# Four score banks shared by all lanes, and softmax numerators formed by a second, transposed product

## The chip, the core and the metric

The kernel runs on one core of a Trainium2 chip. The metric is the time of the whole kernel on the device in microseconds (us), the median of several runs; lower is better. The profile is one further execution, recorded by the hardware profiler. Its engines are named PE (TensorE matmuls), PEld (TensorE weight loads), DVE (VectorE), ACT (ScalarE), POOL (GpSimd) and SP (SyncE, which here issues most DMAs).

## The reference, cut to what matters

Four blocks run one after the other over 32 sequences of 64 tokens with 256 features; every attention has 16 heads of 16 features.

```python
# block 0: queries from x, keys from ctx and x (128 keys), integer key mask on the ctx half
attn = where(full_mask, einsum('bkhd,bnhd->bhkn', q, kmat) / 16, -inf)
x = mlp(rmsnorm(softmax(attn) @ v @ out_w + out_b + x)) + x
# block 1: a recurrent time mix (a scan over 64 steps) and a channel mix; no attention
# block 2: self attention, then cross attention on ctx (64 keys each), then an MLP
scores = einsum('bhqd,bhkd->bhqk', q, k) / 4
scores = scores * mask - 10000.0 * (1.0 - mask)
out = einsum('bhqk,bhkd->bhqd', softmax(scores), v)
# block 3: cross attention with a boolean key mask, gated
scores = where(mask, einsum('bhtd,bhsd->bhts', Q, K) / 4, -inf)
x = x + tanh(gate) * (softmax(scores) @ V @ Wo.T)
```

## The kernel before, in words

The 32 sequences are cut into 8 groups of 4 sequences (256 tokens). A job is one block applied to one group, so there are 32 jobs. Four lanes (class `Lane`, L83) each run one job at a time. A job is a Python generator; the loop at L1235 goes round the lanes and advances each by one `yield`, which sets the priority of the instructions that it emits. A scheduler then places the instructions on each engine's queue by priority and by when it believes that they can start; each queue is worked off in that fixed order. `next_job` (L1194) lets at most two lanes be in block 1, starts block 2 once every group has started block 0, and block 3 once every group has started block 2.

Each lane owns 11 working tiles of 128 x 512 (`s` and `d`) and two of the eight PSUM banks (`BANKS`, L58). Every product that a lane forms takes one of its two banks and gives it back when ACT or DVE has read it. The projections go through `matmul` (L203): most multiply a pair of high and low parts by three products of 128 x 256 (L210), some are plain fp32 (L207).

The 16 heads of an attention are taken as c (2) x r (4) x j (2). The keys are stored block-diagonally: one 32-row strip of the features holds two heads (j), and `bd_keys` (L369) writes each key tile twice, masked by `ind`, so that a product over the strip gives the scores of both heads side by side. The queries hold two strips per 64-row half, and `queries` (L340) writes them twice, each time masked by `par` so that one strip is zero. The product for r then runs over the 64 rows of `half_rows(r)`, half of them zeros.

`attention64` (L449, blocks 2 and 3) makes for each r: a bank of scores (16 fp32 matmuls as PE sees them, L460; in block 3 ahead of them a mask product of two rows, L1161), and `softmax_unit` (L409): a maximum per row over the keys (DVE, L414), a subtraction (DVE, L416), four 128 x 128 transposes (PE, L422), and the exponential (ACT, L424). In block 2 the mask is applied by a DVE multiplication (L1097) and a POOL addition (L1098) ahead of that. The scores of r + 1 are asked for before the unit of r, and there is a `yield` after each r. Then come the sums (L479), the reciprocals, the product with the values (L489) and the output projection. Block 0 does the same inside `block0` (L569) with its own score function (mask product L648, scores L655), sums (L673) and values (L687), twice per job (i = 0, 1). Queries of block 0 are evacuated by four activations (L609). `key_mask` (L549) loads the key mask with one DMA and turns it into 0 or -1e30 in bf16 on two rows.

An attention use is one pass through this for one group (or for one i in block 0). There are 16 uses in block 0, 16 in block 2 and 8 in block 3.

Of the kernel before, what the change touches and what calls it, by code (L numbers as in the profile page):

```python
# [38 lines left out]
ALU = mybir.AluOpType  # L40
# [17 lines left out]
BANKS = (2, 2, 2, 2)  # L58
# [58 lines left out]
def kernel(ctx: ExitStack, tc: tile.TileContext, a: dict, out: bass.AP):  # L117
# [4 lines left out]
    lanes = [Lane(ctx, tc, n) for n in range(NL)]  # L122

# [15 lines left out]
    make_identity(nc, ident)  # L139
    eps5 = mk(const, [P, 1], "eps5")  # L140
# [22 lines left out]
    def feat2(t):  # L163
        return t[:, :512].rearrange("p (c t) -> p c t", c=NC)
# [64 lines left out]
    par = mk(const, [P, 2], "par")  # L229
    nc.scalar.dma_start(out=par, in_=a["par"])  # L230
    half_bf = mk(const, [2, P], "half_bf", dt=BF16)
    halfT = mk(const, [2, P], "halfT")
    nc.scalar.dma_start(out=halfT, in_=a["half"].rearrange("p j -> j p"))
# [106 lines left out]
    def queries(L, w, src, bias):  # L340


        q = [feat2(L.s()) for _ in range(2)]

        def evac(ps):
            for u in range(2):
                on = par[:, u : u + 1]
                if bias is None:
                    nc.scalar.activation(q[u], ps, AF.Copy, scale=on)
                else:  # L350
                    for c in range(NC):
                        nc.scalar.activation(
                            q[u][:, c, :], ps[:, c, :], AF.Identity, bias=bias[:, c, u : u + 1],
                            scale=on,
                        )

        project_T(L, w, src, evac)
        return lambda r, c, seq: q[r % 2][half_rows(r), c, seq * S : (seq + 1) * S]

    def half_rows(r):  # L360
        return slice(64 * (r // 2), 64 * (r // 2) + 64)
# [17 lines left out]
    def keys64(L, w, src, bias):  # L379

        k = [L.d().rearrange("p (b j s) -> p b j s", b=GB, j=2) for _ in range(NC)]
        project_T(
            L, w, src,
            each(lambda c, ps: bd_keys(
                lambda j: k[c][:, :, j, :], ps.rearrange("p (b s) -> p b s", s=S), c, bias
            )),
        )
        return lambda r, c, seq: k[c][half_rows(r), seq].rearrange("p j s -> p (j s)")
# [20 lines left out]
    def softmax_unit(L, s, n, scale, in_place=False):  # L409

        sv = s.rearrange("p (m n) -> p m n", n=n)
        m = 512 // n
        mx = L.tmp([P, m], "mx")
        nc.vector.tensor_reduce(mx, sv, AX.X, ALU.max)  # L414
        d = s if in_place else L.d()
        nc.vector.tensor_tensor(  # L416
            d.rearrange("p (m n) -> p m n", n=n), sv,
            mx.unsqueeze(2).to_broadcast([P, m, n]), ALU.subtract,
        )
        pt = L.bank("T")  # L420
        for i in range(4):
            nc.tensor.transpose(pt[:, i * P : (i + 1) * P], d[:, i * P : (i + 1) * P], ident)  # L422
        e = L.d()
        nc.scalar.activation(e, pt, AF.Exp, scale=scale)  # L424
        return e
# [23 lines left out]
    def attention64(L, q, k, v, scale, masked):  # L449


        def scores(r):
            sc = L.bank("A")
            begun = masked(sc, False)
            for i in range(2):
                for c in range(NC):
                    for b in range(2):
                        seq = 2 * i + b
                        o = (i * NC + c) * P
                        nc.tensor.matmul(  # L460
                            sc[64 * b : 64 * b + 64, o : o + P],
                            lhsT=q(r, c, seq), rhs=k(r, c, seq),
                            start=not begun,
                            stop=not begun or (i, c) == (1, NC - 1),
                        )
            return sc

        es = []
        sc = scores(0)
        for r in range(4):  # L470
            m, own = masked(sc, True), sc

            sc = scores(r + 1) if r < 3 else None
            es.append(softmax_unit(L, m, S, scale, m is not own))
            yield
        out = L.s()[:, :512].rearrange("p (i n) -> p i n", i=TT)
# [54 lines left out]
    def weights0():  # L531
# [4 lines left out]
        W["qb0"] = masked_bias("l0_qb", par)  # L536
# [12 lines left out]
    def key_mask(L, name, g, dt, width):  # L549

        m = L.tmp([2, TT, S], "m2", dt, 1)
        nc.sync.dma_start(
            out=m,
            in_=a[name][g * GB : (g + 1) * GB, :].rearrange("(i b) k -> b i k", b=2),
        )
        f = L.tmp([2, TT, width], "f2", BF16, 1)
        if width > S:
            nc.gpsimd.memset(f[:, :, S:], 0.0)
        nc.vector.tensor_scalar(f[:, :, :S], m, 0.0, -BIG, ALU.is_equal, ALU.mult)
        return f  # L560

# [7 lines left out]
    def block0(L, g):  # L569
        x = tok2(L.s())  # L570
        nc.sync.dma_start(out=x, in_=token_major(a["x"], g))
        mb = key_mask(L, "mask0", g, mybir.dt.int32, 2 * S)
        ct = None
        for i in range(TT):
# [24 lines left out]
            q = L.d().rearrange("p (u c t) -> p u c t", u=2, c=NC)  # L599
# [7 lines left out]
            for u in range(2):  # L607
                for c in range(NC):
                    nc.scalar.activation(  # L609
                        q[:, u, c, :], ps[:, c, :], AF.Identity, bias=W["qb0"][:, c, u : u + 1],  # L610
                        scale=par[:, u : u + 1],
                    )
# [33 lines left out]
            def scores(r):  # L646
                sc = L.bank("A")
                nc.tensor.matmul(  # L648
                    sc.rearrange("p (m n) -> p m n", m=4), lhsT=half_bf,
                    rhs=mb[:, i, :].unsqueeze(1).to_broadcast([2, 4, P]),  # L650
                    start=True, stop=False,
                )
                for c in range(NC):
                    for b in range(2):
                        nc.tensor.matmul(  # L655
                            sc[64 * b : 64 * b + 64, c * D : (c + 1) * D],
                            lhsT=q[half_rows(r), r % 2, c, b * S : (b + 1) * S],
                            rhs=kk[c][half_rows(r), b].rearrange("p j h s -> p (j h s)"),
                            start=False, stop=c == NC - 1,
                        )  # L660
                return sc

            es = []
            sc = scores(0)
            for r in range(4):
                own = sc
                sc = scores(r + 1) if r < 3 else None
                es.append(softmax_unit(L, own, P, 1.0 / DH))
                yield
# [376 lines left out]
    def weights2():  # L1046
# [4 lines left out]
        W["qb2"] = masked_bias("l2_qb", par)  # L1051
# [8 lines left out]
        W["cqb2"] = masked_bias("l2_cqb", par)  # L1060
# [20 lines left out]
    def block2(L, g):  # L1081
        x = load_x(L, g)
        m2 = L.tmp([P, TT, S], "m2", bufs=1)
        nc.sync.dma_start(
            out=m2,
            in_=a["mask2"][g * GB : (g + 1) * GB, 0].rearrange("(i b) q k -> (b q) i k", b=2),
        )
        f2 = L.tmp([P, TT, S], "f2", bufs=1)
        mask_fill(f2, m2)

        def masked(m, f):
            def fn(sc, done):
                if not done:
                    return False
# [279 lines left out]
```

## Time and profile before

| what | value |
|---|---|
| median of 3 runs (lowest to highest) | 1218.55 us (1217.73 to 1218.82) |
| the profiled execution's own time | 1220.28 us |
| its span | 1218.5 us |
| instructions in the span | 26280 |
| mean granted TensorE clock | 0.951 |
| DMA | 69.83 MB, mean 57 GB/s, 18.1% of the 16 engines' time on the main queue |

The span is the stretch of the profile that all shares refer to. In a group line the two numbers after the bar are the summed busy time in us and the mean duration of one in ns; because TensorE overlaps neighbouring matmuls, the busy time of a matmul group divided by its count is the interval at which matmuls follow each other, and it is smaller than the mean duration. After the second bar stands the idle time of the engine just before the group, and what ended it. TensorE counts an fp32 matmul of the source twice, which is why 768 score products in the source are 1536 matmuls in the profile.

### The profile page before, as it was taken

Reading aid. Unit: us, or ns where it says so; the run is one execution under the profiler, and the core shown is the slowest. Engines: PE = TensorE matmul, PEld = TensorE weight load, DVE = VectorE, ACT = ScalarE, POOL = GpSimd, SP = SyncE. Lnnn points to the kernel's source line nnn. Section 1 sums busy time; section 2 is a strip of 40 time slices with the busy share of each in tenths; the row PEclk is TensorE's granted clock in tenths of the full one; section 3 lists DMA queues with packets and bytes.
Section 4 is the critical chain, followed back from the end, with each engine's and each line's share of the span. In section 5 each row is a group of like instructions: output and inputs, shape, how many; then the busy total and the mean of one; then the engine's idle time right before and its main releaser. Section 6 shows DMA issues by size and latency. Waiting matters only on the chain. (4 is left out here: it accounts for less than half of the span.)

```text
span 1218.5 us, 26280 instructions
## 1 busy us (share of the span) xinstructions
PE 1133.0 (93%) x10524; PEld 876.4 (72%) x10524; DVE 875.9 (72%) x1561; ACT 649.5 (53%) x1288; POOL 449.2 (37%) x553
## 2 busy tenths in 40 slices
PE   6999999979998999987889857999999999999998
PEld 5667879746776767765767634897778897788875
DVE  4646563898679877699877997768887455886456
ACT  5556864444464654434634313665557675456852
POOL 2002131542348423366335754455454232231100
PEclk9999998988999999987889886999999999999999
DMA  7300011341122311232221220101000110101101
GB/s 219 112 23 15 27 52 54 122 130 45 53 63 90 102 41 56 61 100 70 90 69 52 76 66 29 45 27 36 21 21 18 37 36 18 45 28 45 61 2 36
DMA packets 76953, 69.83 MB, mean 57 GB/s; under 512 B 10361, under 2 KB 73119, under 8 KB 76831
## 3 DMA queue, kind: packets, MB, share of 16 engines
q1 hardware_dynamic: 76140, 68.10, 18.1%
q8 instruction: 83, 1.36, 0.5%
q14 instruction: 40, 0.32, 0.1%
q10 hardware_dynamic: 690, 0.05, 0.1%
HBM read 49.51 MB, written 14.68 MB: 53 GB/s over the span
## 5 line engine op out<-in xcount | busy, mean ns | idle before, releaser
L210 PE MATMUL bank<-w,s 128*128 128x256 f32 x1632 | 235.8, 292 | 10.3 <-DVE s L200 4.6
L210 PEld LDWEIGHTS bank<-w,s 128*128 128x128 f32 x1632 | 209.1, 192 | 27.9 <-issue 8.8
L210 PE MATMUL bank<-s,w 128*128 128x256 f32 x1344 | 200.3, 297 | 7.5 <-ACT s L199 4.3
L210 PEld LDWEIGHTS bank<-s,w 128*128 128x128 f32 x1344 | 176.5, 197 | 24.8 <-issue 8.1
L424 ACT ACTIVATE s<-bank 128x512 f32<-128x512 f32 x160 | 95.1, 599 | 138.9 <-PE bank L422 127.4
L200 DVE TENSOR_TENSOR s<-s,s 128x512 fp32r<-128x512 f32 x128 | 102.6, 803 | 84.3 <-ACT s L199 83.5
L1098 POOL TENSOR_TENSOR s<-s,f 128x512 f32<-128x512 f32 x64 | 86.6, 1358 | 132.7 <-DVE s L1097 111.5
L207 PE MATMUL bank<-s,w 128*128 128x256 f32 x448 | 114.1, 399 | 2.7 <-DVE s L819 1.3
L960 POOL TENSOR_TENSOR s<-s,s 128x512 f32<-128x512 f32 x64 | 90.1, 1408 | 71.1 <-DVE s L956 67.8
L422 PE MATMUL bank<-ident,s 128*128 128x128 f32 x640 | 105.1, 289 | 6.5 <-DVE s L416 6.1
L460 PE MATMUL bank<-s,s 64*64 64x128 f32 x1536 | 107.7, 278 | 3.3 <-ACT s L424 1.7
L956 DVE TENSOR_TENSOR_SCAN s<-s,s 128x260 f32<-128x260 f32 x128 | 105.8, 867 | 0.5
L199 ACT CAST s<-s 128x512 fp32r<-128x512 f32 x128 | 79.0, 621 | 50.0 <-DVE s L494 31.4
L460 PEld LDWEIGHTS bank<-s,s 64*64 64x64 f32 x1536 | 82.4, 133 | 27.6 <-issue 14.2
L422 PEld LDWEIGHTS bank<-ident,s 128*128 128x128 f32 x640 | 72.8, 145 | 36.6 <-issue 18.8
L207 PEld LDWEIGHTS bank<-s,w 128*128 128x128 f32 x448 | 84.3, 198 | 20.5 <-issue 4.1
L414 DVE TENSOR_REDUCE mx<-bank 128x4 f32<-128x512 f32 (+1 forms) x96 | 65.3, 683 | 40.5 <-PE bank L655 23.4
L869 POOL TENSOR_TENSOR s<-s,s 128x512 f32<-128x512 f32 x40 | 56.2, 1412 | 76.6 <-DVE s L866 58.3
L655 PE MATMUL bank<-s,s 64*64 64x256 f32 x512 | 74.8, 397 | 0.0
L504 ACT ACTIVATE s<-bank,vecs 128x256 f32<-128x256 f32 x128 | 53.7, 472 | 31.2 <-PE bank L210 30.8
L293 ACT ACTIVATE s<-bank,vecs 128x256 f32<-128x256 f32 x96 | 48.8, 567 | 36.1 <-PE bank L258 35.2
L258 PE MATMUL bank<-ident,s 128*128 128x128 f32 x288 | 50.9, 293 | 18.2 <-DVE s L286 10.6
(156 smaller groups left out, 1969.2 us busy)
## 6 DMA issues: line engine op xcount, KB each, us to landing
s<-vd SPq DMA_DIRECT2D x128, 128.0 KB
s<-xd SPq DMA_DIRECT2D x32, 256.0 KB
xd<-s SPq DMA_DIRECT2D x24, 256.0 KB
cxd<-s SPq DMA_DIRECT2D x32, 128.0 KB
s<-cxd SPq DMA_DIRECT2D x16, 256.0 KB
stage<-in_l_w_dram SPq DMA_DIRECT2D x12, 256.0 KB
s<-s SPq DMA_DIRECT2D x48, 64.0 KB
s<-in_x_dram SPq DMA_DIRECT2D x8, 256.0 KB
```

The costliest lines, as they stand in the source:

```text
L199: nc.scalar.copy(hi, src)
L200: (eng or nc.vector).tensor_tensor(lo, src, hi.bitcast(F32), ALU.subtract)
L207: nc.tensor.matmul(out, lhsT=lf(l), rhs=rf(r), start=start, stop=stop)
L210: nc.tensor.matmul(out, lhsT=lf(l[u]), rhs=rf(r[v]), start=start and n == 0, stop=stop and n == 2)
L414: nc.vector.tensor_reduce(mx, sv, AX.X, ALU.max)
L422: nc.tensor.transpose(pt[:, i * P : (i + 1) * P], d[:, i * P : (i + 1) * P], ident)
L424: nc.scalar.activation(e, pt, AF.Exp, scale=scale)
L460: nc.tensor.matmul(sc[64 * b : 64 * b + 64, o : o + P], lhsT=q(r, c, seq), rhs=k(r, c, seq), start=not begun, stop=not begun or (i, c) == ...
L655: nc.tensor.matmul(sc[64 * b : 64 * b + 64, c * D : (c + 1) * D], lhsT=q[half_rows(r), r % 2, c, b * S : (b + 1) * S], rhs=kk[c][half_rows ...
L956: nc.vector.tensor_tensor_scan(f, wT[:, c].rearrange("p b s -> p (b s)"), f, 0.0, ALU.mult, ALU.add)
L960: nc.gpsimd.tensor_tensor(st, st, per_t(rT[:, c, :]), ALU.mult)
L1098: nc.gpsimd.tensor_tensor(sv, sv, f, ALU.add)
```

## The change

Each lane keeps one PSUM bank of its own, and the other four banks become one tile `sc` that all lanes share. An attention takes the tile whole, and the next user waits until the last one has read it.

The masking of the queries by `par` is gone: the queries are written once, and the product for r runs over its own 32-row strip (`pair_rows`). The four r are the innermost loop, each writing its own bank of `sc`, so that neighbouring matmuls use different strips of rows and different halves of columns of the array.

In blocks 0 and 3 the subtraction, the transposes and the reading of scores for them are gone. Instead `maxima` reduces two banks at a time on DVE, `shifts` splits each maximum into three bf16 parts with four small POOL operations and turns them by one product, which ACT copies to SBUF; `numerators` writes the same four banks again: the mask, the scores with keys and queries exchanged (so that they come out transposed), and the product of `take_off` (a constant of minus ones) with the parts, which takes the maxima off. Then four exponentials read the banks. There are three yields where there were five.

In block 2 all four r are multiplied and masked first, then reduced, subtracted and transposed as before, but into a second use of the shared tile. Its mask tile is loaded later, into a working tile.

`key_mask` now writes the mask to four strips by four DMAs, and the constants for it (zeroed tiles per lane, `half_bf` on four strips, `take_off`, `parts`) are made at the start.

```diff
-BANKS = (2, 2, 2, 2)
+BANKS = (1, 1, 1, 1)
...
+    score_ps = ctx.enter_context(tc.tile_pool(name="score_ps", bufs=1, space=PSUM))
...
     def queries(L, w, src, bias):
-        q = [feat2(L.s()) for _ in range(2)]
+        q = feat2(L.s())
...
+    def score_banks():
+        return mk(score_ps, [P, 4, 512], "sc")
+
+    def maxima(L, mx, src, n):
+        nc.vector.tensor_reduce(mx, src.rearrange("p r (m n) -> p r m n", n=n), AX.X, ALU.max)
+
+    def shifts(L, mx):
+        t = parts[L.n]
+        wide = lambda m: m.to_broadcast([P, 4, 4, 2]) if m.shape[3] == 1 else m
+        rest = L.tmp([P, 4, 4, 2], "rest", bufs=1)
+        nc.gpsimd.tensor_copy(t[:, :, 0], wide(mx))
+        nc.gpsimd.tensor_tensor(rest, wide(mx), t[:, :, 0], ALU.subtract)
+        nc.gpsimd.tensor_copy(t[:, :, 1], rest)
+        nc.gpsimd.tensor_tensor(t[:, :, 2], rest, t[:, :, 1], ALU.subtract)
+        ps = L.bank("T")[:, :P]
+        nc.tensor.matmul(
+            ps, lhsT=t.rearrange("p r u m j -> p (r u m j)"), rhs=ident_bf, start=True, stop=True
         )
+        sh = L.s(BF16)[:, :P]
+        nc.scalar.copy(sh, ps)
+        return sh
+
+    def numerators(L, sc, sh, q, k, scale, mask):
+        for m in range(4):
+            o = m * P
+            for r in range(4):
+                nc.tensor.matmul(
+                    sc[:, r, o : o + P], lhsT=mask(r, m), rhs=half_bf[32 * r : 32 * r + 2],
+                    start=m == 0, stop=False,
+                )
+        for m in range(4):
+            for b in range(2):
+                o = m * P + b * S
+                for r in range(4):
+                    nc.tensor.matmul(
+                        sc[:, r, o : o + S], lhsT=k(r, m, b), rhs=q(r, m, b),
+                        start=False, stop=False,
+                    )
+        for m in range(4):
+            o = m * P
+            for r in range(4):
+                nc.tensor.matmul(
+                    sc[:, r, o : o + P], lhsT=take_off[32 * r : 32 * r + 24, m],
+                    rhs=sh[32 * r : 32 * r + 24], start=False, stop=m == 3,
+                )
+        es = [L.d() for _ in range(4)]
+        for r, e in enumerate(es):
+            nc.scalar.activation(e, sc[:, r], AF.Exp, scale=scale)
+        return es
...
+    def attention64(L, q, k, v, scale, masked=None, key_masks=None):
+        sc = score_banks()
+        if key_masks is not None:
+            begin_masked(
...
+        for i in range(2):
+            for c in range(NC):
+                o = (i * NC + c) * P
+                for b in range(2):
+                    for r in range(4):
                         nc.tensor.matmul(
-                            sc[64 * b : 64 * b + 64, o : o + P],
-                            lhsT=q(r, c, seq), rhs=k(r, c, seq),
+                            sc[64 * b : 64 * b + 64, r, o : o + P],
+                            lhsT=q(r, c, 2 * i + b), rhs=k(r, c, 2 * i + b),
...
+        if key_masks is not None:
+            for r in range(0, 4, 2):
+                maxima(L, mx[:, r : r + 2], sc[:, r : r + 2], S)
+            sh = shifts(L, mx.rearrange("p r (m j) -> p r m j", j=2))
             yield
+            es = numerators(
...
+        else:
+            ds = [masked(sc[:, r]) for r in range(4)]
+            yield
+            for r, d in enumerate(ds):
+                dv = d.rearrange("p (m n) -> p m n", n=S)
+                nc.vector.tensor_reduce(mx[:, r], dv, AX.X, ALU.max)
+                nc.vector.tensor_tensor(
+                    dv, dv, mx[:, r].unsqueeze(2).to_broadcast([P, 8, S]), ALU.subtract
+                )
+            pt = score_banks()
+            es = []
+            for r, d in enumerate(ds):
+                for m in range(4):
+                    nc.tensor.transpose(
+                        pt[:, r, m * P : (m + 1) * P], d[:, m * P : (m + 1) * P], ident
+                    )
+                es.append(L.d())
+                nc.scalar.activation(es[r], pt[:, r], AF.Exp, scale=scale)
+        yield
...
+    def key_mask(L, name, g, dt, both):
...
+        for r in range(4):
+            nc.sync.dma_start(
+                out=m[32 * r : 32 * r + 2],
...
+    def begin_masked(sc, mask, n):
+        for b in range(2):
+            for r in range(4):
+                nc.tensor.matmul(
+                    n(sc[64 * b : 64 * b + 64, r]),
+                    lhsT=half_bf[32 * r : 32 * r + 2, 64 * b : 64 * b + 64],
+                    rhs=mask(r), start=True, stop=False,
+                )
```

Block 0 takes the same route: `begin_masked`, scores over `pair_rows(r)` with r innermost, `maxima`, `shifts`, a yield, `numerators`, a yield.

## The prediction

> **What bounds the kernel now.** I read the page's first two parts first, to see which engine is full and where.
>
> ```profile
> PE 1133.0 (93%) x10524; PEld 876.4 (72%) x10524; DVE 875.9 (72%) x1561; ACT 649.5 (53%) x1288; POOL 449.2 (37%) x553
> PE   6999999979998999987889857999999999999998
> PEclk9999998988999999987889886999999999999999
> ```
>
> TensorE has work in 93% of the span. The kernel has stages, so I then asked for the busy time of each engine in six stretches (PE, PEld, DVE, ACT, POOL, then clock, DMA share, GB/s):
>
> ```profile
> 30.00:200.00 170.00, 168.57 (x1689) 125.34 (x1685) 93.61 (x173) 108.92 (x221) 27.00 (x47) 0.99 0.16 45
> 200.00:330.00 130.00, 120.92 (x844) 86.21 (x845) 98.71 (x172) 58.30 (x119) 50.21 (x63) 0.89 0.28 86
> 330.00:550.00 220.00, 208.30 (x1654) 154.51 (x1653) 176.42 (x303) 105.56 (x215) 108.14 (x125) 0.97 0.24 74
> 550.00:765.00 215.00, 176.43 (x1331) 130.93 (x1331) 184.36 (x299) 91.38 (x173) 111.32 (x120) 0.84 0.20 64
> 765.00:950.00 185.00, 178.30 (x1919) 149.40 (x1919) 138.42 (x263) 114.23 (x224) 92.45 (x100) 0.99 0.09 28
> 950.00:1198.00 248.00, 246.90 (x2746) 203.47 (x2745) 158.12 (x297) 149.97 (x295) 53.63 (x72) 0.99 0.11 33
> ```
>
> From 30 to 200 and from 765 to 1198 us TensorE is full (99% and 98%) and nothing else is near it: time taken off TensorE there comes off the end. Between 200 and 765 us block 1 runs, DVE is at 76 to 86%, TensorE has gaps and its granted clock drops.
>
> Last, the groups that the change touches, and two pieces of the chain that ended last:
>
> ```profile
> L460 PE MATMUL bank<-s,s 64*64 64x128 f32 x1536 | 107.7, 278 | 3.3 <-ACT s L424 1.7 <-DVE s L1097 1.3
> L422 PE MATMUL bank<-ident,s 128*128 128x128 f32 x640 | 105.1, 289 | 6.5 <-DVE s L416 6.1
> L655 PE MATMUL bank<-s,s 64*64 64x256 f32 x512 | 74.8, 397 | 0.0
> L416 DVE TENSOR_TENSOR s<-bank,mx 128x512 f32<-128x512 f32 x96 | 65.4, 684 | 1.9
> L489 PE MATMUL bank<-s,s 128*32 128x64 f32 x1536 | 38.7, 226 | 0.0
> L950 POOL COPY s<-s0T 128x8 f32<-128x8 f32 x64 | 28.7, 455 | 26.1 <-DVE s L932 7.3 <-PE bank L210 6.3 <-PE bank L963 4.7
> L648 PE MATMUL bank<-f,half_bf 2*128 2x512 bf16 x64 | 24.6, 384 | 2.7 <-ACT s L424 2.6
> L1161 PE MATMUL bank<-f,half_bf 2*128 2x512 bf16 x32 | 12.1, 384 | 0.0
> ...
> 811.99 1.95 PE bank L460 x41
> 976.95 1.89 PE bank L460 x32
> ```
>
> Busy over count is the interval between matmuls: 70 ns for L460, 146 for L655, 164 for a transpose (L422), 25 for L489, whose neighbours use four column strips. The chain's two lines say that strips of rows run side by side too: 32 score matmuls took 1.89 us, 41 took 1.95. In the longer run neighbours come from both 64-row halves.
>
> **The scores in eight tiles.** Per use, from the rows:
> - Block 0: 4 x 0.384 (L648) + 32 x 0.146 = 6.2 us. Now 8 mask products and 32 score matmuls.
> - Block 3: 4 x 0.378 (L1161) + 64 x 0.070 = 6.0. Now 8 + 64.
> - Block 2: 64 x 0.070 = 4.5. Now 64.
>
> The interval over eight tiles is not in the trace. Bounds: 109 ns (a pair of L460 in step) over 8, or 14 ns, and L489's 25 to 27, which may be a floor of issue. I take 27, as L489 is the nearest row. With 0.15 to 0.3 us for filling and changing tiles that gives 1.4, 2.2 and 1.9 us, so 4.8 x 16 + 3.8 x 8 + 2.6 x 16 = 149 us off TensorE. At 14 ns it would be 27 more.
>
> **The numerators for the transposes.** Out: 16 x 0.164 = 2.6 us. In: 16 mask products, 64 score matmuls of 64 columns and 16 products with take_off, all over four row strips, at 27 ns 2.6 us, and 0.3 for the turning product and changes of tile: +0.3 x 24 = +7. TensorE together: **-142 us**.
>
> Here a rule speaks against the change. The Trainium skill, page "TensorE: Matmul & The Clock Gate", section "LDWEIGHTS (loading the stationary operand)", says that a load's time goes with its columns and not with its rows, columns over 1.2 ns. The transposed scores load 128 columns for only 32 rows: 107 ns each as an estimate by the page, 64 per use. One after the other that is 5.1 us more per use, +123 us in all. The records inside the run at 811.99 speak for overlap: a load of the second row half started 3 ns after one of the first, and its first matmul took 320 ns instead of 269, so it waited for one load of 64 columns (51 ns), not two. I take overlap and keep +123 as the other end.
>
> **The waits that take the place.** TensorE's order is fixed, so a matmul that waits holds all behind it, every lane's. I counted in the changed kernel's order what stands ahead of each wait, at the durations of before.
> - The numerators' first product waits for two maxima. A reduction of two banks: 0.683 us for 512 elements, plus 512 more at 1.08 ns (L494 against L694: 697 and 420 ns for 512 and 256) = 1.24; two with hand-offs 3.0 us. Ahead stand 2.6 us at the median; the shortfalls over 24 uses sum to 17 us (13 at 2.7 us, 29 at 3.7).
> - The turning product waits for four POOL operations in a row: by L950 some 0.4 us each, with hand-offs 2.0. Ahead stand only 0.6 us at the median: 39 us in all. At 1.2 us (L272's 245 ns each) it is 22; at 3.4, queued behind one of POOL's 1.4 us operations, 70. I take 17 + 39 = **+56**; the bounds are +35 and +99.
> - One bank per lane: 581 uses of a lane's own bank, each of which can start only when the one before was read. Against 1.5 us for reading and hand-offs (two of L504 at 472 ns and 0.5) the shortfalls sum to 50 us, against 2.0 us to 105. TensorE's 85 us of idle time already hold some such waits: I take **+25**, with 0 and 105 as bounds.
> - The sums and the next user of the shared banks wait for four exponentials (4 x 0.6): shortfalls 7 to 13 us, I take **+8**.
>
> **Start.** The first thing in TensorE's queue becomes a mask product that needs half_bf, which was ready at 7.9 us by one DMA and now takes four; the first transposes ran at 4.46. SP also issues four mask DMAs, behind POOL's memsets, ahead of ctx. **+4**. Later, 48 more DMAs at 0.35 us of SP time each stand ahead of other lanes' loads; those are issued well ahead of use, so 0 (17 if none were hidden).
>
> **Off the path.** DVE loses 96 x 0.684 (L416) and, in reductions, 96 x 0.683 against 48 x 1.24: -71 us. ACT loses half of the query evacuations (-33) and gains 24 small copies and six table loads of 1.28. POOL gains 24 x 1.6 = 38. None is full in the full stages, so none counts; what hides them is TensorE's own work, and DVE has 76 us to spare even in 30 to 200.
>
> **What of this reaches the end.** Eight uses of block 0 lie between 200 and 550 us and four of block 2 before 765. There I let half of the saving count: 8 x 4.5 / 2 + 4 x 2.6 / 2 = +23 given back, and likewise 14 us of the waits not felt. With less work and more gaps the clock will be lower in more stretches (0.84 where TensorE was at 82%): +10, bounds 0 and 30.
>
> Sum: -142 + 56 + 25 + 8 + 4 + 23 - 14 + 10 = -30. Against the profiled execution's own 1220.3 us: 1190; the median of the runs stands 1.7 below that execution, so **1189**.
>
> **The rivals.**
> - The covers hold: other lanes fill every wait, and only the work counts: -142 + 23 + 4 = -115, **1104**. For it: median covers of 2.6 to 3.5 us, more than one evacuation. Against: the order gives the POOL chain 0.6 us.
> - Slower, by one bank per lane: where before a lane's next product began while its last was being read, each of 581 uses waits for ACT's or DVE's queue, which are busy 53 to 72% of the time, so a read takes 2 us or more. Price 105 instead of 25: +50, **1269**. It decides from 55 us, or 95 ns per use. For it: four busy queues between products; against: median 3 us of other lanes' work in between.
> - The row strips do not overlap as meant (the rule above): +123, of which some 24 lie in the wait for POOL: -30 + 99, **1288**. For it: no four-strip run exists in the trace; against: the run of 41.
>
> **How the numbers follow.** The sum's own case 0.35 (1150 to 1216), covers hold 0.20, no change 0.05, one bank 0.28, strips 0.12. The range 1105 to 1280 reaches into the outer cases and leaves out about half of the first and most of the last. A measurement of this kernel can tell about 0.2% from no change. Faster 0.55, same 0.05, slower 0.40.
>
> **What would show it.** Right: score matmuls near 27 ns by busy over count, numerators under 3 us per use, TensorE busy near 990 us, idle of 1 to 2 us ahead of the turning product, released by POOL. Wrong: 100 ns per transposed score matmul (strips); idle ahead of L210's successors released by ACT and DVE summing to over 100 us (one bank); TensorE as full as before (the work did not fall); a clock under 0.9.

## The result and the profile after

| kernel | median us (lowest to highest) | ratio to before, 95% interval | profiled execution: own time, span |
|---|---|---|---|
| before | 1218.14 (1213.93 to 1218.82), 4 runs | | 1220.28, 1218.5 |
| changed | 1317.75 (1310.70 to 1322.59), 4 runs | 1.0807 (1.0763 to 1.085) | 1322.59, 1320.8 |

The changed kernel is 8% slower, outside the predicted range. Its page, first the shares, then the two slice rows of TensorE:

```profile
PE 1129.5 (86%) x12564; PEld 858.5 (65%) x12564; DVE 821.0 (62%) x1430; ACT 625.5 (47%) x1246; POOL 485.1 (37%) x658
PE   4799899968899878896879898589998878999997
PEclk9699898956999987898889998799999979998887
```

TensorE is busy for as long as before (1129.5 us, 1133.0 before), although groups of 324 us (scores, masks, transposes) gave way to groups of 231; its idle time rose from 85.5 to 191.3 us. So the span grew by 102 us: idle time grew by 106, and busy time fell by 3.5. The mean clock fell from 0.951 to 0.900: the records have the clock at one half for 265 us, against 122 before.

The busy time by stretch, with the bounds used before where a stage has kept its place (columns as before: PE, PEld, DVE, ACT, POOL, clock, DMA share, GB/s):

```profile
30.00:200.00 170.00, 146.08 (x2248) 112.82 (x2248) 65.35 (x124) 93.56 (x202) 31.46 (x74) 0.90 0.17 48
200.00:330.00 130.00, 111.62 (x820) 85.44 (x822) 77.46 (x112) 44.31 (x90) 48.54 (x61) 0.74 0.27 83
330.00:550.00 220.00, 194.50 (x2161) 149.70 (x2162) 139.47 (x257) 113.31 (x224) 87.84 (x122) 0.91 0.17 53
950.00:1300.00 350.00, 316.08 (x4129) 238.90 (x4128) 192.23 (x340) 179.06 (x355) 91.89 (x132) 0.94 0.10 31
```

The stretches in which TensorE was full before (99% from 30 to 200 us, 98% at the end) are now at 86% and 90%, at a clock of 0.90 and 0.94. No other engine took its place: DVE is at 38% and 55% there.

The groups that stand where L460, L422, L655, L648, L1161 and L479 stood:

```profile
L562 PE MATMUL bank<-s,ones_bd 128*32 128x512 f32 x192 | 91.5, 635 | 4.0 <-ACT s L557 3.3 <-ACT s L482 0.7
L469 PE MATMUL sc<-s,s 32*128 32x64 f32 x1536 | 71.7, 313 | 0.0
L523 PE MATMUL sc<-s,s 32*64 32x128 f32 x1536 | 40.9, 281 | 0.0
L761 PE MATMUL sc<-s,s 32*64 32x256 f32 x512 | 26.0, 405 | 0.1
L476 PE MATMUL sc<-s,take_off 24*128 24x128 bf16 x384 | 15.9, 246 | 0.2 <-ACT s L452 0.2
L461 PE MATMUL sc<-half_bf,kf 2*128 2x128 bf16 x384 | 13.2, 229 | 14.0 <-DVE mx L436 14.0
```

Scores (L523, L761) are cheap as meant: 26.6 and 51 ns each by busy over count (L761 streams 256 columns, L523 128). The numerators' products (L469) stand at 47 ns, not 27. The sums (L562), whose code nobody had touched, went from 254 to 476 ns each; the line of before:

```profile
L479 PE MATMUL bank<-s,ones_bd 128*32 128x512 f32 x192 | 48.7, 631 | 0.9 <-ACT s L424 0.9
```

What TensorE waits for: four lines of its table of waits (us in total, times, longest):

```profile
PE bank L1072 <- POOL s L1069: 35.0, 22, 4.9
PE sc L461 <- DVE mx L436: 14.0, 12, 2.5
PE bank L448 <- POOL parts L446: 8.3, 12, 1.3
PE bank L782 <- ACT s L482: 7.8, 4, 6.1
```

The largest is in block 1 (L1072 was L963, with 11.5 us before), which the change touches only by giving its lane one bank. The waits that the change adds to the attention are, taken together, no larger than predicted. The gaps lie in many small places, so the table alone does not name the cause.

### The profile page after: what moved, and what is told of

The parts are those of the page before. It is cut to its first block, busy times and chain, and to the rows that moved or that the text cites. A ratio compares the mean times of both kernels' runs of the same rounds, so it can differ in the third digit from the quotient of the medians.

```text
span 1320.8 us, 30426 instructions
## 1 busy us (share of the span) xinstructions
PE 1129.5 (86%) x12564; PEld 858.5 (65%) x12564; DVE 821.0 (62%) x1430; ACT 625.5 (47%) x1246; POOL 485.1 (37%) x658
## 5 line engine op out<-in xcount | busy, mean ns | idle before, releaser
L233 PE MATMUL bank<-w,s 128*128 128x256 f32 x1632 | 240.9, 299 | 14.2 <-DVE s L223 6.5
L233 PEld LDWEIGHTS bank<-w,s 128*128 128x128 f32 x1632 | 214.3, 198 | 45.1 <-issue 13.2
L233 PE MATMUL bank<-s,w 128*128 128x256 f32 x1344 | 211.0, 308 | 18.0 <-DVE s L223 6.8
L233 PEld LDWEIGHTS bank<-s,w 128*128 128x128 f32 x1344 | 185.0, 206 | 48.1 <-issue 18.4
L230 PE MATMUL bank<-s,w 128*128 128x256 f32 x448 | 114.0, 400 | 8.5 <-DVE s L975 4.1
L230 PEld LDWEIGHTS bank<-s,w 128*128 128x128 f32 x448 | 84.5, 198 | 27.0 <-issue 6.4
L562 PE MATMUL bank<-s,ones_bd 128*32 128x512 f32 x192 | 91.5, 635 | 4.0 <-ACT s L557 3.3
L436 DVE TENSOR_REDUCE mx<-sc 128x8 f32<-128x1024 f32 (+1 forms) x48 | 56.4, 1216 | 46.2 <-PE sc L523 32.4
L1072 PE MATMUL bank<-s,heads 128*32 128x256 f32 x256 | 47.2, 500 | 35.0 <-POOL s L1069 35.0
L298 POOL TENSOR_SCALAR rstd<-bnmv 128x2 f32<-128x2 f32 x48 | 12.2, 253 | 175.7 <-DVE bnmv L307 174.2
L469 PE MATMUL sc<-s,s 32*128 32x64 f32 x1536 | 71.7, 313 | 0.0
L469 PEld LDWEIGHTS sc<-s,s 32*128 32x128 f32 x1536 | 64.3, 223 | 7.7 <-issue 5.6
L312 DVE TENSOR_SCALAR s<-s,bnmv,rstd 128x256 f32<-128x256 f32 x96 | 49.1, 552 | 30.5 <-POOL rstd L299 27.7
L284 PE MATMUL bank<-ident,s 128*128 128x128 f32 x288 | 49.9, 293 | 17.2 <-DVE s L312 12.9
```

Source lines behind the costliest of these rows:

```text
L230: nc.tensor.matmul(out, lhsT=lf(l), rhs=rf(r), start=start, stop=stop)
L233: nc.tensor.matmul(out, lhsT=lf(l[u]), rhs=rf(r[v]), start=start and n == 0, stop=stop and n == 2)
L284: nc.tensor.transpose(ps[:, c, i * P : (i + 1) * P], src[:, i, c * P : (c + 1) * P], ident)
L436: nc.vector.tensor_reduce(mx, src.rearrange("p r (m n) -> p r m n", n=n), AX.X, ALU.max)
L469: nc.tensor.matmul(sc[:, r, o : o + S], lhsT=k(r, m, b), rhs=q(r, m, b), start=False, stop=False,)
L562: nc.tensor.matmul(sums[32 * r : 32 * r + 32, :], lhsT=ones_bd, rhs=es[r], start=True, stop=True)
```

## The experiments

The numbers are medians of four runs or more, with the ratio to the kernel before and its 95% interval. The forms by themselves come from a single run. The theories weighed: (a) each lane with one bank is a chain, and TensorE's gaps grow; (b) the new steps of the attention (POOL chain, numerators, strips) cost what was saved; (c) it is the work or clock of TensorE.

### One bank in block 1 alone

The kernel before with the two banks of a lane named apart and taken in turn; in `b1_one`, block 1 takes the first only.

```diff
 def bank(self, tag):
-    return self._tile(self.ps, [P, 512], "bank", BANKS[self.n], F32)
+    self.turn = 0 if self.one else 1 - self.turn
+    return self._tile(self.ps, [P, 512], f"bank{self.turn}", 1, F32)
...
 def block1(L, g):
+    L.one = ONE        # True in b1_one, False in b1_two
...
+    L.one = False      # at the end of block 1
```

> The kernel before, with one thing taken away: while a lane runs block 1 it may use only one of its two PSUM banks (blocks 0, 2 and 3 alternate between both). Theory 'block 1 sets the pace, and one bank per lane makes its chain longer': the pairs of block 1 jobs, 165 us apart in the kernel before, come 170 to 180 us apart, and the kernel takes 1280 to 1330 us. Rival 'the shared score banks hold the lanes up': no change beyond the control, 1210 to 1235 us.

> Control of the kernel with one bank in block 1: the same code, with both banks in block 1 too. Both theories: as the kernel before, 1210 to 1230 us; a difference is what a slightly different order of the schedule costs.

Measured: 1252.96 us, 1.0267 (1.0224 to 1.0311), against 1211.36 us, 0.9922 (0.9898 to 0.9946), for the control. One bank costs 41.6 us in this stage alone, on unchanged work. The wait of block 1's product for POOL went from 7.4 to 27.9 us, much as in the changed kernel (11.5 to 35.0). The first line is of one bank, the second of the control:

```profile
PE bank L968 <- POOL s L965: 27.9, 20, 2.5
```

```profile
PE bank L968 <- POOL s L965: 7.4, 7, 2.0
```

Taking the banks strictly in turn is by itself 0.8% faster than before.

### Block 1 left out

Both kernels with block 1's job replaced by a load and a store, so its computation is left out.

```diff
-    blocks = [block0, block1, block2, block3]
+    blocks = [block0, block1_out, block2, block3]
```

> The kernel before with the computation of block 1 left out (its rows are loaded and stored unchanged; its weights are still loaded). It is the base for the changed kernel without block 1. TensorE has about 1133 us of work less some 150 for block 1; without the pace of block 1 it should be full: 880 to 1000 us by both theories.

> The changed kernel with the computation of block 1 left out in the same way. Theory 'the loss sits in block 1's chain': faster than the kernel before without block 1, by 40 to 110 us. Rival 'the shared score banks or the waits in TensorE's queue': slower than it, by 30 to 100 us.

Measured: 908.12 us (904.83 to 911.34) and 983.65 us (980.60 to 985.66): 75.5 us of the loss remain. The first line below is of the kernel before without block 1, the second of the changed one:

```profile
PE 873.4 (96%) x9356; PEld 694.7 (77%) x9356; DVE 560.3 (62%) x1017; ACT 543.8 (60%) x1110; POOL 222.0 (25%) x313
```

```profile
PE 844.6 (86%) x11396; PEld 659.8 (67%) x11396; DVE 495.1 (50%) x886; ACT 528.4 (54%) x1074; POOL 250.1 (25%) x418
```

So block 1 is not the only place. In the other blocks the work falls by 29 us, and idle time rises from 33 to 138 us with no engine full. So what holds TensorE up there is the lanes' own chains or the shared tile, not a full engine.

### The sums given their overlap back

```diff
-        for r in range(4):
+        for r in (3, 2, 1, 0):      # the sums of both attentions
```

The exponentials end in the order 0 to 3. Asked for in that order, each sum starts alone and waits for the next exponential; asked for in reverse, all four wait once and then run side by side.

> The changed kernel with the four products for the sums in the order r = 3, 2, 1, 0 (and so in block 0), so that the first waits for the last exponential and all four follow each other in four column strips. Theory 'part of the loss is that the sums are issued one by one as exponentials finish, and lose their overlap': the interval of the sums goes from 476 ns back to about 254, TensorE's busy time falls by 40 us or more, and the kernel takes 1270 to 1295 us. Rival 'the sums only fill gaps that are there anyway': within 10 us of 1318.

Measured: 1325.48 us, 1.0847 (1.0798 to 1.0895).

```profile
PE 1076.8 (81%) x12564; PEld 859.7 (65%) x12564; DVE 821.5 (62%) x1430; ACT 645.7 (49%) x1262; POOL 482.2 (36%) x658
```

```profile
L562 PE MATMUL bank<-s,ones_bd 128*32 128x512 f32 x192 | 28.8, 677 | 7.5 <-ACT s L557 4.9 <-ACT s L482 2.4
```

L562 fell from 91.5 to 28.8 us and TensorE's busy time by 53 us; the time did not fall. In the changed kernel TensorE's work no longer sets the end: what is taken off turns into idle time (191 to 247 us), and the clock falls further, to 0.881. The new order adds waits of its own ahead of the sums and the next user's scores and masks (L562, L782, L523, L664), but they come to only some 14 us of the 56.

### The shared tile by halves

The r in two pairs, each pair in a shared tile of two banks. `shared2_once` has one such tile (two banks of PSUM lie unused), `shared2_twice` two, `shared2_lanes2` one, and a second bank for lanes 0 and 1.

```diff
-    return mk(score_ps, [P, 4, 512], "sc")
+    return mk(score_ps, [P, 2, 512], "sc", SHARED)
...
-        for r in range(4):
+        for r in (h, h + 1):
```

> The changed kernel with the r taken in two pairs, and a shared tile of two banks instead of four; one bank per lane, two banks left unused. It is the base for the next two. By both theories 1310 to 1380 us: four tiles side by side give the scores the same 27 ns as eight, the numerators over two row strips some 55 ns; if it is not slower than the changed kernel, the size of the shared tile doesn't matter.

> As the base with the shared tile of two banks, but with two such tiles, so that two users hold scores at once; one bank per lane. Theory 'lanes queue for the shared banks': 50 us or more faster than the base, under 1280. Rival 'one bank per lane': within 20 us of the base.

> As the base with one shared tile of two banks, but lanes 0 and 1 have two banks of their own (lanes 2 and 3 one). Theory 'one bank per lane': 30 to 60 us faster than the base (two of four lanes relieved). Rival 'lanes queue for the shared banks': within 20 us of the base.

Measured: 1434.38, 1400.67 and 1420.83 us (1.1751, 1.1477, 1.1635). More banks help in either place (34 us for two banks as a second shared tile, 14 us for two as second banks of two lanes). By the ranges set beforehand this is nearer to lanes queueing for the shared tile than to single banks: 34 lies between the two theories (50 or more, within 20), and 14 lies in the range of the queue (within 20) and not in that of single banks (30 to 60). All three are far slower than the changed kernel: with two strips instead of four the numerators' products take 83 to 89 ns instead of 47. So they are no clean split of the changed kernel's own loss, as they change strips and banks together.

### The POOL chain, the numerators and the rate of the lanes

`after_const_shift` leaves out the POOL operations, the turning product and its copy, and multiplies `take_off` with zeros: the maxima aren't subtracted in blocks 0 and 3, and the exponent's scale is made tiny. `after_transposes` undoes the numerators; `after_yields` goes back to five yields.

```diff
 # after_const_shift, in shifts
-        nc.gpsimd.tensor_copy(t[:, :, 0], wide(mx))
...
-        return sh
+        return parts0
 # after_transposes, in place of shifts and numerators
+        for r, d in enumerate(es):
+            nc.vector.tensor_tensor(
+                d.rearrange("p (m n) -> p m n", n=n),
+                sc[:, r].rearrange("p (m n) -> p m n", n=n),
+                mx[:, r].unsqueeze(2).to_broadcast([P, 512 // n, n]), ALU.subtract,
+            )
+        pt = score_banks()
+        for r, d in enumerate(es):
+            for m in range(4):
+                nc.tensor.transpose(pt[:, r, m * P : (m + 1) * P], d[:, m * P : (m + 1) * P], ident)
+            nc.scalar.activation(d, pt[:, r], AF.Exp, scale=scale)
 # after_yields
-        yield
+        for _ in range(3):
+            yield
```

> The changed kernel with the four POOL operations, the turning product and its copy left out: take_off is multiplied with a constant tile of zeros, the maxima are still reduced, and the exponent's scale is made tiny so that sums stay finite; the maxima are not subtracted in blocks 0 and 3. The numerators now wait for the two reductions alone. Prediction's own term for this chain: 39 us, so about 1279. Theory (the hold of the shared tile is the bound, this chain is 2 to 3 us of each of 24 holds): 1250 to 1285 us. Rival (the gaps come from the lanes' single banks, the chain lies beside other work): 1305 to 1320 us.

> The changed kernel with the numerators undone: blocks 0 and 3 subtract the maxima on DVE and transpose into a second use of the shared tile, as block 2 does; shared tile, strips and single banks stay. TensorE works some 44 us less than in the changed kernel (107 us of numerators against 63 of transposes), DVE 65 us more, and the shared tile is taken 24 times more often. Theory (shared tile and single banks are what costs): 1300 to 1345 us. Rival (the numerators and their waits are what costs): 1230 to 1275 us.

> The changed kernel with five yields per attention instead of three, so that the lanes go round at the rate of before; same instructions, other order. Theory (the holding of shared and single banks limits, not the rate at which lanes are advanced): 1305 to 1330 us, as the changed kernel's 1318. Rival (attentions crowd each other because three yields let a lane run through its attention in fewer rounds): 1260 to 1295 us.

Measured: 1311.41 us, 1.0735 (1.07 to 1.077); 1363.23 us, 1.1141 (1.1111 to 1.1172); 1331.08 us, 1.0876 (1.084 to 1.0913). Taking the POOL chain out whole gives 6 us, so it lies beside other waits: the theory that its 2 to 3 us per hold are on the path falls. Going back from the numerators to transposes makes it 45 us slower, above what either theory expected. That run takes the shared tile 24 times more, so it does not give the price of the numerators alone; it shows that they are not what makes the changed kernel slower than transposes in the same shared tile. The rate at which lanes are advanced is no cause: more yields give no gain.

### The strips alone, and the clock

`pairs_own` is the kernel before with the queries written once and 32-row strips, the r two at a time in the lane's own two banks; `own_32` has the strips without the pairs, `pairs_64` the pairs without the strips.

```diff
-        return lambda r, c, seq: q[r % 2][half_rows(r), c, seq * S : (seq + 1) * S]   # pairs_own, own_32
+        return lambda r, c, seq: q[pair_rows(r), c, seq * S : (seq + 1) * S]
...
-                        nc.tensor.matmul(                                             # pairs_own, pairs_64
-                            sc[64 * b : 64 * b + 64, o : o + P],
+                        for r, sc, on in zip(rs, scs, begun):
+                            nc.tensor.matmul(
+                                sc[64 * b : 64 * b + 64, o : o + P],
...
```

> The kernel before with only the query part of the change: queries written once, scores over 32-row strips, the r taken two at a time in the lane's own two banks; no shared tile, transposes as before. Theory (the saving is real, and lost by the shared tile and the one bank): score matmuls near 50 ns by busy over count for the 128-column ones (70 before) and near 90 for the 256-column ones (146), so 50 to 60 us less TensorE work, TensorE still over 90% busy, 1160 to 1200 us. Rival (holding both own banks at once costs what the work saves): 1215 to 1260 us with idle time ahead of the transposes and the next scores.

> The kernel before with one thing changed: queries written once and score products over 32-row strips instead of 64 rows half of which are zeros; order, banks and transposes as before. The products stream as many columns as before. Theory (the clock follows the rows in use): the granted clock falls from 0.95 to about 0.91, half-clock time from some 120 us to over 200, and the time rises to 1240 to 1270 us, though ACT has less to do and no bank is held longer. Rival (the clock follows idle time): clock 0.945 to 0.96, 1205 to 1225 us.

> The twin of it: scores of two r at a time in the lane's own two banks as in pairs_own, but over 64 rows with masked queries, as before. Theory (the clock follows the rows in use): clock near 0.95, 1205 to 1240 us, the rest of pairs_own's loss being rows. Rival (holding both banks costs what pairs_own lost): 1255 to 1285 us.

Measured: 1270.44 us, 1.0362 (1.0308 to 1.0416); 1252.51 us, 1.0257 (1.0196 to 1.0318); 1236.15 us, 1.0144 (1.01 to 1.0187). The profiled execution of `pairs_own` was its longest run (1280.7 us), so the argument rests on `own_32`. Its page:

```profile
PE 1160.1 (92%) x10524; PEld 893.5 (71%) x10524; DVE 879.0 (70%) x1555; ACT 618.1 (49%) x1215; POOL 451.4 (36%) x553
PEclk9579998988999989988879867999999999989989
```

The products stream as many columns as before and ACT has 31 us less to do, yet it is 33 us slower at a clock of 0.918. The records carry the clock in steps of 3.413 us. In the kernel before, 3 of 21 drops to half clock follow a step in which TensorE was busy for over 90%; in `own_32` it is 11 of 27. So narrow products can lower the clock with TensorE busy. In the changed kernel it is only 3 of 30: there 25 drops follow a step under 60% busy, and such steps rose from 22 to 52. So its clock falls with its gaps.

### The forms by themselves

No job of the kernel is left, only bursts of one form each, all operands ready, with full products (128 rows and columns) between them.

```diff
...
+    for burst in (
+        lambda: full(60),
+        lambda: eight_tiles(640), lambda: full(60),
+        lambda: four_strips(360), lambda: full(60),
+        lambda: one_strip(240, 32), lambda: full(60),
+        lambda: one_strip(240, 64), lambda: full(60),
+        lambda: one_strip(240, 128), lambda: full(60),
+        lambda: two_rows(120), lambda: full(60),
+    ):
+        burst()
```

> No job of the kernel is left: after the constants, seven bursts of 60 full fp32 products (128 rows, 128 columns, 128 moving) with one burst of another form between each two: 640 products in eight tiles 32x64; 360 in four strips 32x128 with 64 moving columns; 240 in two column halves over 32, 64 and 128 rows; 120 bf16 products of two rows by 512 columns. All operands are ready, so TensorE is never idle. Theory (the clock follows the rows in use): full clock in the full bursts, half clock within 3.4 to 7 us in the bursts of 2 rows, of 32 rows and of four strips (row share under 0.25), full clock for 128 rows and probably for 64 and for eight tiles (row share about 0.5). Rival (the clock follows busy time): full clock throughout.

The stretches in order: eight tiles, full products, four strips, 32 rows, 64 rows, 128 rows, two rows (PE, PEld, DVE, POOL, then the clock):

```profile
20.00:53.00 33.00, 18.76 (x1175) 16.72 (x1159) 0.00 (x0) 0.00 (x0) 1.00 0.02 4
54.00:67.00 13.00, 13.00 (x118) 13.00 (x118) 0.00 (x0) 0.00 (x0) 1.00 0.01 3
70.00:88.00 18.00, 17.79 (x632) 17.57 (x629) 0.00 (x0) 0.00 (x0) 1.00 0.02 5
107.00:148.00 41.00, 41.00 (x389) 41.00 (x387) 0.00 (x0) 0.00 (x0) 0.50 0.01 1
166.00:189.00 23.00, 23.00 (x427) 23.00 (x423) 0.00 (x0) 0.00 (x0) 1.00 0.01 3
206.00:229.00 23.00, 23.00 (x426) 23.00 (x424) 0.00 (x0) 0.00 (x0) 1.00 0.01 2
247.00:291.00 44.00, 44.00 (x104) 14.99 (x102) 0.00 (x0) 0.00 (x0) 0.50 0.00 0
```

TensorE is 100% busy with one strip of 32 rows and with two rows, and the clock is at one half; the 32-row products then take 97 ns each instead of 55 for 64 or 128 rows. Four strips and eight tiles keep full speed: expected at half, the four strips were a miss. So rows in use seem to count over all strips at work. The burst of eight tiles adds a limit to what was said of gaps: TensorE was busy for only 57% of its 33 us, and the clock stayed full, so a busy share under 60% is no threshold by itself. The Trainium skill, page "TensorE: Matmul & The Clock Gate", section "What's actually happening", says that the gate goes by how busy TensorE has been recently; the bursts of one strip and of two rows were wholly busy and were gated, so here the measurement decides: rows in use weigh too.

### Full rows added to the numerators

```diff
+    zero_bf = mk(const, [P, P], "zero_bf", dt=BF16)
+    nc.gpsimd.memset(zero_bf, 0.0)
...
+            if m % 2 == 0:
+                for r in range(2):
+                    nc.tensor.matmul(
+                        sc[:, r].rearrange("p (m n) -> p m n", m=4), lhsT=zero_bf,
+                        rhs=ident_bf.unsqueeze(1).to_broadcast([P, 4, P]),
+                        start=False, stop=False,
+                    )
```

> The changed kernel with more work: among the numerators of blocks 0 and 3, four products of 128 rows by 512 columns with a tile of zeros are added per use into the same banks (they add zero), 96 in all, some 20 us of TensorE and up to 20 us of changes of tile. Theory (narrow products starve the clock): half-clock time falls from 265 us by 40 to 100 us, the numerators' score products from 47 ns towards 35 ns, and the time is not higher and may be lower: 1280 to 1318 us. Rival (the clock follows idle time alone, work is work): clock as before, 1325 to 1355 us.

Measured: 1364.59 us, 1.1186 (1.1116 to 1.1257), clock 0.897, half-clock time 285 us. The added products took 36.1 us and the time rose by 47: the theory that narrow numerators starve the clock in the changed kernel falls, as the count of drops had it. Work added inside a hold of the shared tile (from a use's first product to its last reading) was on the path, at its price and more.

### One bank per lane everywhere

The kernel before with the scores of r + 1 asked for after the unit of r, with two banks (`late_two`, the control) and with one (`late_one`, four banks unused). No shared tile, no strips.

```diff
-        sc = scores(0)
         for r in range(4):
-            m, own = masked(sc, True), sc
-
-            sc = scores(r + 1) if r < 3 else None
+            own = scores(r)
+            m = masked(own, True)
...
-BANKS = (2, 2, 2, 2)
+BANKS = (1, 1, 1, 1)      # late_one
```

> Control: the kernel before, but the scores of r + 1 are asked for after the unit of r instead of ahead of it; two banks per lane. Both theories: 1215 to 1245 us, clock about 0.95.

> The same program with one bank per lane in all stages (four banks unused), no shared tile, 64-row scores, transposes. Theory (one bank per lane makes the gaps): 60 to 110 us above the control, clock 0.90 to 0.92, TensorE's idle time 150 us or more. Rival (the shared tile makes them; one bank costs only the 41 us seen in block 1, or the prediction's 25): 25 to 50 us above the control, clock 0.93 or more.

Measured: 1251.31 us, 1.0268 (1.0232 to 1.0303), and 1312.18 us, 1.0779 (1.073 to 1.0828). The first line is of the control, the second of one bank:

```profile
PE 1152.7 (92%) x10524; PEld 881.4 (70%) x10524; DVE 883.5 (71%) x1561; ACT 642.9 (51%) x1280; POOL 452.4 (36%) x553
```

```profile
PE 1145.6 (88%) x10524; PEld 880.6 (67%) x10524; DVE 890.9 (68%) x1561; ACT 619.6 (47%) x1265; POOL 456.8 (35%) x553
```

The same instructions with one bank: +61 us, all of it idle time (98 to 160 us), and steps under 60% busy went from 22 to 41 (the clock from 0.938 to 0.917). It is at the lower end of what theory (a) asked; the rival's 25 to 50 us falls. Scores not asked for ahead cost another 34 us (1251.31 against 1217.3 for the kernel before, measured beside it). With both, the kernel before, with all its old work, stands at 1312 us, within 6 us of the changed kernel.

The places of the loss do not agree, though. Take the first and the last product of block 1's scan (L963 of before, L1072 of after) as marks. `late_one` reaches the first 47 us later than its control (280 us against 233) and needs only 7 us more after the last (495 against 488). The changed kernel reaches the first 30 us later than before (261 against 231), and after the last it takes 458 us for 1439 projection products (L233) that are left, where the kernel before took 471 us for 1740 (L210). The stretch after the last, `late_one` first, then the changed kernel:

```profile
811.00:1306.00 495.00, 454.44 (x5172) 379.44 (x5160) 334.57 (x619) 271.31 (x542) 155.26 (x181) 0.98 0.10 30
```

```profile
863.00:1321.00 458.00, 408.56 (x5116) 308.44 (x5114) 266.63 (x477) 227.50 (x450) 137.38 (x184) 0.94 0.09 29
```

So one bank per lane, as this pair has it, does not explain what the changed kernel loses in its last stage, and the two totals agree in part by chance. In that stage its shared tile is held for 80% of the time, and over the eight uses of block 3 at the end for 87%, each 10 to 33 us long, one after the other.

## Why the prediction was wrong, point by point

- **Scores in eight tiles (27 ns, -149): right in sum.** 26.6 ns for L523; block 0's products (L761, 256 columns) take 51 and the masks (L664) 75, which the sum put at 27 as well. L523, L761 and the masks (14.5 us) sum to 81 us for the 219 of before: -138.
- **The row strips overlap: right.** The estimate of 107 ns per transposed score product did not come: in the bursts four strips run at 29 ns each, so their loads ran side by side.
- **Numerators (+7): mis-sized.** L469, L476, L461 and the turning product sum to 107 us for 63 us of transposes: +44. Split by the recorded clock, L469 takes 37 ns at full speed and 75 at half by busy over count, and 406 of 1536 fall into half clock.
- **TensorE together (-142): measured -94** in these groups. What the sum left out: the sums lost their overlap (L562 and its twin in block 0: 78 to 127 us, +49), the values went down by 17, the groups that nobody touched went up by 23 at the lower clock. These come to -39; the busy time of the whole fell by just 3.5, so the other 35 are neighbours of different groups that overlap less. In this account the whole miss lies in TensorE's busy time: -132 was predicted with the clock's +10, and -3.5 came.
- **Waits: their sum was right by luck, their parts not.** The terms that are idle time (56, 25, 8, 4, 23 and -14) came to 102; the trace has 106. The maxima were right (14.0 us for 17). The POOL chain was put at 39: TensorE waits 8.3 us for it, and without it the time is 6 us less. One bank per lane was put at 25: the control pair shows 61. The exponentials: 8 predicted, 11.8 waited. The start was right: 4 predicted; the first product comes at 12.5 us (it waits for the mask, L653) instead of 4.5, but idle time in the first 30 us grew by only 4.7 us.
- **The step that failed: what of the saved work reaches the end, with the clock at +10.** The sum took the gaps as additions to a TensorE that still sets the end, and subtracted the work from it. After the change TensorE's work no longer sets the end: 53 us less of it gave nothing (the sums put last). Waits between the lanes' steps do, by their single banks, the shared tile or both: the work of before with one bank and late scores is as slow in total. Gaps of this kind went with a lower clock, too: 122 us at half became 265. Two terms of the sum were also mis-sized, the numerators (+44 for +7) and the sums' lost overlap (+49, put at nothing).
- **The rival "slower, by one bank per lane" (0.28, 1269) had the direction, and its mechanism is real in the old attention.** Its price of 105 was above what the control pair shows (61, past its deciding point of 55; that pair also takes its own banks for scores and transposes, so the price is not one for the same 581 uses). It fell 49 us short; it still subtracted the saved work and put the clock at 10. That single banks are what slows the changed kernel as a whole is not shown: the places of the loss differ.
- **What would show it:** the sign of "wrong" that came is TensorE busy for as long as before (1129.5 us, not near 990); the clock, at 0.900, stands at the edge of its sign. Numerators took 4.5 us per use, not under 3. The sign set for one bank, over 100 us of idle time ahead of the successor of L210, did not come: L233 has 32 us, against 18 before. The idle time has no one large releaser.

Open: how the loss divides between the shared tile and the single banks in the changed kernel itself. That late scores (34) and one bank (61) add up to 95 of its 100 us is an account on the old attention, not a proof for the new one, and it loses in other places. For the shared tile speak that it is held for 89% of the time from 30 to 200 us (TensorE is busy for 86%) and that a second one gave 34 us with tiles of two banks; against it, that 2 to 3 us taken out of 24 holds gave 6 us in all. A hold also grows when TensorE works for other lanes meanwhile, so a full tile is not yet the cause. The direct test, the shared tile with two banks per lane, needs 12 banks and could not be tried. No version tried beats both kernels by more than the 0.8% of the banks taken in turn.

## What to carry to other kernels

Banks let TensorE, whose order is fixed, work while a result is being read: before you spend them on wider tiles, run the old kernel with the banks that will be left, which gives a first price without the rewrite (61 us here). Then compare where the two lose time, not only their totals. Work taken off the full engine counts only as long as it stays the full one; when a change adds waits to every lane, ask what bounds the lanes then, and do not count on a saving there. Deal narrow products over all row strips: from one strip alone they lowered the clock here, from four in turn they did not.

## What the runs showed of the hardware

- The clock went by rows in use as well as by busy time: one strip of 32 rows, 100% busy, ran at half clock from 5 us after its start (97 ns each for 55); 64 rows did not.
- Eight tiles of 32x64 by themselves take 16 ns each (20.8 us busy for 1280), with nine pauses of 1.3 to 2.2 us between starts, put down to issue, that no semaphore explains; with these it is 27.6. In the kernel it was 26.6.
- Two strips of rows asked for in turn did not pay (1270 us): in the longest run of `pairs_own` its products stand at 60 ns (92.4 us for 1536) against 70 before, and those of 256 columns at 168 against 146, at a lower clock (0.902).
- Sums over four column strips took 254 ns each in the kernel before, 476 when each is released singly, and 150 (28.8 us for 192) when all four wait for the last exponential and then run together.
